# Two stored blocks to a product and a shorter ring of gathers in the second layer of a relational graph network

## The chip, the cores and the metric

The kernel runs on one core of one Trainium2 chip. The metric is the device time of one execution in microseconds (us). A profile is one execution taken by the hardware profiler. The core's engines work side by side and wait for each other through semaphores: TensorE (PE; PEld is its loading of weights), VectorE (DVE), ScalarE (ACT), GpSimd (POOL), and SyncE (SP), which only issues transfers here. POOL issues the indirect transfers, the gathers.

## The reference

12,500 nodes with 128 features, 200,000 edges sorted by their destination. An edge's relation, one of ten, is the argmax of ten of its attributes. Each of two layers takes, for each node and relation, the mean of the features of the edges' sources, projects it with the relation's matrix, adds the ten, and adds the projected node itself and a bias. The result is added to x and normalised.

```
def _rgcn_layer(x, src, dst, edge_type, w_rel, root, bias):
    seg = dst * NUM_REL + edge_type
    sums = segment_sum(x[src], seg, N * NUM_REL)
    cnt = segment_sum(ones, seg, N * NUM_REL)
    mean = (sums / maximum(cnt, 1.0)[:, None]).reshape(N, NUM_REL, -1)
    return einsum('nrd,rdo->no', mean, w_rel) + x @ root + bias
h = relu(_rgcn_layer(x, src, dst, edge_type, w_rel1, root1, b1))
out = layernorm(x + _rgcn_layer(h, src, dst, edge_type, w_rel2, root2, b2))
```

## The kernel before

Edges are taken in 1563 tiles of 128, in the order of their destinations. For a tile, POOL gathers the 128 source rows by an indirect transfer (`gathered`, L833), DVE builds a one-hot matrix with the edges' weights (`hots`, L840), PE multiplies the two into PSUM, and DVE adds the result to a running accumulator at a register's offset.

Layer 1 walks all tiles (products at L1077, additions at L866). As blocks of 256 nodes are finished, it writes their rows, projected with layer 2's ten matrices, to YD, and their features to hT. While it goes it also sums, for edges whose source's layer-1 row is ready, layer 2's sums by relation; they are stored for each block in SD. Its gathers of two rows at once use four buffers of four places each: the ring is 16 tiles long and is refilled in pieces of four.

Layer 2 (`layer_2`) handles the remaining edges from the projected rows in YD: 177 plain tiles, and 678 tiles of edges brought together from all over by a sort on the chip (`brought_together`, `listed`), whose steps are interleaved with the 177 plain tiles as jobs due at a tile's number. The tiles are walked in bunches of up to four. For bunch p the program emits, in this order: one-hots for bunch p + 3 (AH), blocks to be begun (`begun`, the product with root, L1499), gathers of the bunch (L833), its products (L1607), with a call of `between.run` after each tile's product, jobs, the additions of bunch p - 2 (L1637), and finished blocks (`finish`: transposes L1540, norm L773 to L783, rows out). Each engine executes its part in that order.

Two things inside this walk matter here.

The ring of gathers: `gathers` has six buffers of GQ = 8 places, so 48 tiles. Each time eight tiles have been gathered, the next buffer is taken. The order of places within a buffer is turned round at every second use, so that the first gather of a buffer waits for the last product that read it; that one wait covers the eight.

The stored sums: a block of 256 nodes whose sums are in SD is called heavy; there are 46. For each, `seen_in` loads SD's ten slices into one of two `held` tiles (L1513, issued by SP), and `seen` spreads ten products, one a relation, over the walk (L1521, up to 256 columns, into the one PSUM bank `alone`), then adds the bank to the layer's accumulator (L1528). A heavy block takes 12 tiles of the walk: products at 0 to 6, the addition at 9. The load for the block after the next is issued when the tenth product is done. A block is finished only when its tiles are done and its stored sums are added.

Of the kernel before, what the change touches and what calls it, by code (L numbers as in the profile page):

```python
# [21 lines left out]
NREL = 10  # L22
# [7 lines left out]
QB = 4  # L30
GB = 6
OB = 7
GQ = 8
# [13 lines left out]
BN = 2 * P  # L47
# [5 lines left out]
LAST = 40  # L53
READY = 5
NEAR = 4
GAPW = 112
LOW = 1 << 13
TOPN = (1 << 14) - 1
# [10 lines left out]
def rgcn_resnorm_kernel(ctx: ExitStack, tc: tile.TileContext, x, src, dst, attr, w_rel1, root1, b1,  # L69
# [7 lines left out]
    nc = tc.nc  # L77
# [130 lines left out]
    groups2, u = [], 0  # L208
    while u < NT2:
        n, w = group_at(u, UX if u < UX else NT2)  # L210
# [15 lines left out]
    SD = dram.tile([C, NREL, N], F32, name="SD")  # L226
# [8 lines left out]
    gathers = [lasting.tile([P, GQ * C], F32, name=f"g{i}") for i in range(GB)]  # L235
# [4 lines left out]
    def next_of(kind, of):  # L240

        turn_of_[kind] += 1
        return of[(turn_of_[kind] - 1) % len(of)]
# [98 lines left out]
    at = [0]  # L342
# [15 lines left out]
    first = float(chunk_rows(NCH - 1) * P) - 0.5  # L358
# [13 lines left out]
    n = chunk_rows(NCH - 1)  # L372
# [124 lines left out]
    wsb, rsb, bsb = [], [], []  # L497
# [635 lines left out]
    for a in range(0, NREL * RW, YB):  # L1133
        m = min(NREL * RW - a, YB)
# [33 lines left out]
    every = cc.rearrange("p l r n -> p (l r n)")  # L1168
# [250 lines left out]
    def layer_2():  # L1419
# [53 lines left out]
        heavy = [k for k in finals if block(k)[0] + block(k)[1] > first_sum]  # L1473
        opening = issued[plain - AH]
        due_at = [issued[max(0, first_at[k] - AH - 2)] for k in range(NB2)]
        for j, k in enumerate(heavy):
            due_at[k] = min(due_at[k], opening + 12 * j - 12)
        begin = sorted(range(NB2), key=lambda k: (due_at[k], k))
        xs = [comp.tile([P, 2, C], F32, name=f"x{i}") for i in range(3)]
        vs = [every[:, FIRST - 4 * BN:FIRST - 3 * BN].rearrange("p (t c) -> p t c", c=C)]  # L1480
        os_ = [comp.tile([P, 2, C], F32, name=f"o{i}") for i in range(2)]
        hs = [every[:, FIRST - (i + 1) * BN:FIRST - i * BN] for i in range(3)]
        held = [every[:, i * NREL * BN:(i + 1) * NREL * BN].rearrange("p (r n) -> p r n", r=NREL) for i in range(2)]
        turn_of_.update(x=0, v=0, o=0, h=0, sd=0)
        xbs, fTs, sds = {}, {}, {}
        whole, alone = set(), []
# [16 lines left out]
        def rows_in_turn(j):  # L1503
            if j < NB2:
                xbs[finals[j]] = next_of("x", xs)
                rows_dma(xbs[finals[j]], x, finals[j], False)

        def seen_in(j):
            if j < len(heavy):
                k = heavy[j]  # L1510
                n0, n, _ = block(k)
                sds[k] = next_of("sd", held)
                nc.sync.dma_start(sds[k][:, :, :n], SD[:, :, n0:n0 + n])  # L1513

        def seen(j, i):
            k = heavy[j]
            n0, n, _ = block(k)
            po = alone[0]

            def one(r):  # L1520
                nc.tensor.matmul(po[:, :n], wsb[1][:, r, :], sds[k][:, r, :n], start=(r == 0), stop=(r == NREL - 1))  # L1521
                if r == NREL - 1:
                    sds.pop(k)
                    seen_in(j + 2)

            def added(_):
                assert k in begin[:begins]
                nc.vector.tensor_tensor(acc2[:, n0:n0 + n], acc2[:, n0:n0 + n], po[:, :n], op=ALU.add)  # L1528
                whole.add(k)
            for r in range(NREL):  # L1530
                between.at(i + 2 * r // 3, lambda _, r=r: one(r))
            between.at(i + 9, added)

        def finish(j):
            k = finals[j]
# [24 lines left out]
        used_ = {}  # L1560
# [5 lines left out]
        for p in range(-AH, NB + BE):  # L1566
            if p == plain - AH:
                assert wanted[0] in ready
                masking.close()
                ps_n = fast.enter_context(tc.tile_pool(name="ps_n", bufs=1, space=PSUM))  # L1570
                banks[:] = [next_of("zp", banks) for _ in banks] + [ps_n.tile([P, YB], F32, name=f"zq{j}") for j in range(2)]
                turn_of_["zp"] = 0
                alone.append(ps_n.tile([P, YB], F32, name="alone"))
                for j in range(len(heavy)):
                    seen(j, i + 6 + 12 * j)
            if p + AH < NB:
                second, t0, n, w = bunches[p + AH]
                keys, weights = (keyB, wB) if second else (keyE, wE)
# [9 lines left out]
            if p < NB:  # L1588
                second, t0, n, w = bunches[p]
                oh = ohs.pop(p)  # L1590
                zps[p] = zp = next_of("zp", banks)
                for j in range(n):
                    if made % GQ == 0:
                        g = next_of("g", gathers)
                        turn = used_[id(g)] = 1 - used_.get(id(g), 1)
                    at = GQ - 1 - made % GQ if turn else made % GQ
                    made += 1
                    t = t0 + j
                    if second:
                        gathered(g, at, YD[:, :], idxB[:, t:t + 1], 1)  # L1600
                    else:
                        gathered(g, at, YD[:NREL * (limit_of(t) + 1), :] if t >= T0 else YD[:, :], idxE[:, t:t + 1], 1)
                    gs[j] = g, at
                for j in range(n):
                    g, at = gs.pop(j)
                    o = 0 if second else j * w
                    nc.tensor.matmul(zp[:, o:o + w], g[:, at * C:(at + 1) * C], oh[:, j * w:(j + 1) * w],  # L1607
                                     start=not second or j == 0, stop=not second or j == n - 1)
                    between.run(issued[p] + j + 1)
                i = issued[p + 1]  # L1610
# [204 lines left out]
```

## Time and profile before

| | us |
|---|---|
| runs (median of 3) | 3691.79 (3684.78 to 3692.25) |
| profiled execution | 3655.59 |
| its span | 3653.8 |
| POOL busy in the span | 2294.6 (63%) |
| PE busy in the span | 2254.1 (62%) |
| DVE busy in the span | 1994.0 (55%) |
| mean granted TensorE clock | 0.753 |

A row of the profile names the line, the engine, the operation, the tile written and those read, and the shape; behind it, the count and the times. In a timeline the first two numbers are the start and the length in us; a bracket gives how long the engine stood idle before, and what ended that ("issue": nothing that the profile shows; "remote": something that it could not tell). A product of float32 leaves two records. A gather is POOL's record DMA_INDIRECT; its length is that of the issue, not of the transfer.

### The profile page before, as it was taken

The page shows a single profiled execution, that of the slowest core. Times are in us where ns is not written, and L with a number is a line of the kernel's source. Part 1 is how long each engine was busy: PE and PEld are TensorE (multiplying, and loading weights), DVE is VectorE, ACT ScalarE, POOL GpSimd, SP SyncE. Part 2 cuts the span into 40 slices and gives each one's busy share as a digit, 9 for nine tenths or more (in the row PEclk, how much of TensorE's full clock was granted, in tenths as well). Part 3 has the DMA queues.
Part 4 walks back from the last instruction along what each step waited for, and adds up shares of the span by engine and source line. Part 5 has one row for each costly group of instructions (what it writes and reads, how often), then busy time and mean ns, then how long its engine had stood idle before and what let it go on. Part 6 is the DMA issues. An engine that isn't in the chain of part 4 may idle for free. (4 is left out here: it accounts for less than half of the span.)

```text
span 3653.8 us, 38569 instructions
## 1 busy us (share of the span) xinstructions
PE 2254.1 (62%) x11125; PEld 1859.4 (51%) x11125; DVE 1994.0 (55%) x6434; ACT 514.6 (14%) x799; POOL 2294.6 (63%) x2430
## 2 busy tenths in 40 slices
PE   1556677677676767676667667733556566566534
PEld 0445565565555555555555555623445555555433
DVE  4646576867565757565656565428654333233333
ACT  1111121212121212122212121100000000000000
POOL 5663666666666666666666666566566666666664
PEclk7677877878888888887888877855667777677655
DMA  4553656555555555555656555531144444444322
GB/s 122 154 170 96 189 155 192 153 186 165 172 172 169 172 177 176 171 182 158 191 159 194 158 161 157 146 98 51 46 117 135 143 137 140 136 151 135 97 61 51
DMA packets 376423, 529.31 MB, mean 145 GB/s; under 512 B 55904, under 2 KB 283707, under 8 KB 376204
## 3 DMA queue, kind: packets, MB, share of 16 engines
q0 software_dynamic: 99552, 249.45, 23.9%
q1 hardware_dynamic: 249209, 264.48, 22.4%
q10 hardware_dynamic: 27443, 12.82, 1.2%
q8 instruction: 93, 1.52, 0.2%
q14 instruction: 126, 1.03, 0.1%
HBM read 372.75 MB, written 160.19 MB: 146 GB/s over the span
## 5 line engine op out<-in xcount | busy, mean ns | idle before, releaser
L833 POOL DMA_INDIRECT g<-XH,idxE x1386 | 1314.1, 948 | 737.7 <-issue 364.8
L1077 PEld LDWEIGHTS zp<-oh,g 128*128 128x128 f32 x5898 | 901.7, 229 | 407.3 <-DVE cc L866 201.5
L1077 PE MATMUL zp<-oh,g 128*128 128x120 f32 x5898 | 943.1, 317 | 247.3 <-DVE cc L866 159.0
L866 DVE TENSOR_TENSOR cc<-cc,zp 128x240 f32 (+1 forms) x1563 | 607.1, 388 | 787.1 <-remote 353.0
L833 POOL DMA_INDIRECT g<-YD,idxB x678 | 642.6, 948 | 339.8 <-issue 185.9
L934 PE MATMUL yb<-w,a 128*128 128x512 f32 (+1 forms) x576 | 345.2, 689 | 346.0 <-ACT ys L940 183.1
L840 DVE TENSOR_SCALAR oh<-bank,keyE,wE 128x120 f32<-128x120 f32 x1563 | 517.7, 394 | 0.0
L1521 PE MATMUL alone<-cc,w 128*128 128x256 f32 (+2 forms) x920 | 339.4, 485 | 136.4 <-DVE cc L1528 72.8
L1607 PEld LDWEIGHTS zy<-oh,g 128*128 128x128 f32 x1168 | 245.9, 273 | 222.5 <-DVE cc L1637 155.1
L1607 PE MATMUL zy<-oh,g 128*128 128x12 f32 (+30 forms) x1168 | 237.2, 330 | 197.3 <-DVE cc L1637 148.2
L940 ACT ACTIVATE ys<-yb 128x512 f32<-128x512 f32 (+2 forms) x291 | 153.0, 526 | 1334.4 <-remote 553.7
L934 PEld LDWEIGHTS yb<-w,a 128*128 128x128 f32 x576 | 110.8, 240 | 379.1 <-ACT ys L940 203.6
L1521 PEld LDWEIGHTS alone<-cc,w 128*128 128x128 f32 x920 | 195.3, 247 | 158.3 <-DVE cc L1528 76.5
L826 PE MATMUL pf<-cc,w 128*128 128x256 f32 (+2 forms) x1040 | 248.4, 396 | 15.1 <-issue 9.2
L833 POOL DMA_INDIRECT g<-in_x_dram,idxE x177 | 167.8, 948 | 135.7 <-PE zp L1077 59.3
L833 POOL DMA_INDIRECT g<-YD,idxE x177 | 168.6, 953 | 111.1 <-issue 60.6
L826 PEld LDWEIGHTS pf<-cc,w 128*128 128x128 f32 x1040 | 205.7, 212 | 49.3 <-issue 19.8
L795 ACT ACTIVATE cc<-zero 128x1280 f32<-128x1280 f32 x170 | 214.6, 1262 | 0.0
L840 DVE TENSOR_SCALAR oh<-columns,keyB,wB 128x45 f32<-128x45 f32 (+35 forms) x678 | 177.0, 336 | 0.2 <-issue 0.2
L1637 DVE TENSOR_TENSOR cc<-cc,zy 128x12 f32 (+24 forms) x306 | 58.9, 192 | 177.8 <-remote 145.5
L1607 PEld LDWEIGHTS zq<-oh,g 128*128 128x128 f32 x542 | 113.2, 258 | 30.8 <-issue 18.4
L1528 DVE TENSOR_TENSOR cc<-cc,alone 128x256 f32<-128x256 f32 (+2 forms) x46 | 18.6, 405 | 199.3 <-remote 159.0
(265 smaller groups left out, 1563.5 us busy)
## 6 DMA issues: line engine op xcount, KB each, us to landing
SD<-cc SPq DMA_DIRECT2D x41, 1280.0 KB
cc<-SD SPq DMA_DIRECT2D x41, 1280.0 KB
YD<-ys SPq DMA_DIRECT2D x194, 256.0 KB
m<-in_edge_attr_dram SPq DMA_DIRECT2D x48, 672.0 KB
g<-XH,idxE POOLq DMA_INDIRECT x1386
YD<-ys SPq DMA_DIRECT2D x97, 128.0 KB
XH<-hb SPq DMA_DIRECT2D x44, 256.0 KB
g<-YD,idxB POOLq DMA_INDIRECT x678
```

The costliest lines, as they stand in the source:

```text
L795: nc.scalar.activation(cc[:, l, h * H:(h + 1) * H, o:o + n], zero[:, None, :n].to_broadcast([P, H, n]), AF.Copy)
L826: nc.tensor.matmul(po[:, :n], wsb[l][:, r, :], sums[:, r], start=(r == 0), stop=(w is None and r == NREL - 1))
L833: nc.gpsimd.indirect_dma_start(out=g[:, j * C:(j + n) * C], out_offset=None, in_=table, in_offset=bass.IndirectOffsetOnAxis(ap=idx, axis=0))
L840: nc.vector.tensor_scalar(oh[:, j * m:(j + 1) * m], cols[:, :m], keys[:, j:j + 1], weights[:, j:j + 1], op0=ALU.is_equal, op1=ALU.mult)
L866: nc.vector.tensor_tensor(s, s, z, op=ALU.add)
L934: nc.tensor.matmul(yb[:h, :m], fin_a[k][:, b * P:b * P + h], wsb[1][:, r:r + m // C, :], start=True, stop=True)
L940: nc.scalar.activation(ys[:h, :m], yb[:h, :m], AF.Copy)
L1077: nc.tensor.matmul(zp[:, o + l * KW:o + (l + 1) * KW], g[:, (slot[j] + l) * C:(slot[j] + l + 1) * C], oh[:, j * KW:(j + 1) * KW], start=Tr ...
L1521: nc.tensor.matmul(po[:, :n], wsb[1][:, r, :], sds[k][:, r, :n], start=(r == 0), stop=(r == NREL - 1))
L1528: nc.vector.tensor_tensor(acc2[:, n0:n0 + n], acc2[:, n0:n0 + n], po[:, :n], op=ALU.add)
L1607: nc.tensor.matmul(zp[:, o:o + w], g[:, at * C:(at + 1) * C], oh[:, j * w:(j + 1) * w], start=not second or j == 0, stop=not second or j = ...
L1637: nc.vector.tensor_tensor(s, s, zps[q][:, j * w:(j + 1) * w], op=ALU.add)
```

## The change

In layer 2, adjacent heavy blocks are put into groups of up to 512 columns whose first tiles lie less than 60 apart. One load of SD, ten products and one addition now serve a group; `held` tiles are twice as wide. A group takes 24 tiles of the walk: products at 0 to 13, the addition at 19. And the gathers use only the first two buffers, each as two pieces of four places: the ring is 16 tiles long and is refilled in pieces of four, with the same turning of the order.

```
+PACE = 24
+APART = 60
...
-        for j, k in enumerate(heavy):
-            due_at[k] = min(due_at[k], opening + 12 * j - 12)
+        pairs = []
+        for k in sorted(heavy, key=lambda k: block(k)[0]):
+            if pairs and block(pairs[-1][0])[0] + 2 * BN >= sum(block(k)[:2]) and first_at[k] - first_at[pairs[-1][0]] < APART:
+                pairs[-1].append(k)
+            else:
+                pairs.append([k])
+        pairs.sort(key=lambda u: min(finals.index(k) for k in u))
+        for j, u in enumerate(pairs):
+            for k in u:
+                due_at[k] = min(due_at[k], opening + PACE * j - 12)
...
-        held = [every[:, i * NREL * BN:(i + 1) * NREL * BN].rearrange("p (r n) -> p r n", r=NREL) for i in range(2)]
+        held = [every[:, 2 * i * NREL * BN:2 * (i + 1) * NREL * BN].rearrange("p (r n) -> p r n", r=NREL) for i in range(2)]
...
+        def span_of(j):
+            return block(pairs[j][0])[0], sum(block(k)[1] for k in pairs[j])
...
             def one(r):
-                nc.tensor.matmul(po[:, :n], wsb[1][:, r, :], sds[k][:, r, :n], start=(r == 0), stop=(r == NREL - 1))
+                nc.tensor.matmul(po[:, :n], wsb[1][:, r, :], sds[j][:, r, :n], start=(r == 0), stop=(r == NREL - 1))
...
             for r in range(NREL):
-                between.at(i + 2 * r // 3, lambda _, r=r: one(r))
-            between.at(i + 9, added)
+                between.at(i + 3 * r // 2, lambda _, r=r: one(r))
+            between.at(i + PACE - 5, added)
...
-                for j in range(len(heavy)):
-                    seen(j, i + 6 + 12 * j)
+                for j in range(len(pairs)):
+                    seen(j, i + 6 + PACE * j)
...
-                    if made % GQ == 0:
-                        g = next_of("g", gathers)
-                        turn = used_[id(g)] = 1 - used_.get(id(g), 1)
-                    at = GQ - 1 - made % GQ if turn else made % GQ
+                    if made % QB == 0:
+                        m = made // QB % NEAR
+                        g, first = gathers[m // 2], m % 2 * QB
+                        turn = used_[m] = 1 - used_.get(m, 1)
+                    at = first + (QB - 1 - made % QB if turn else made % QB)
```

More of the change, by code (lines that the diff above doesn't have):

```diff
@@ L1482, in layer_2 @@
         hs = [every[:, FIRST - (i + 1) * BN:FIRST - i * BN] for i in range(3)]
-        held = [every[:, i * NREL * BN:(i + 1) * NREL * BN].rearrange("p (r n) -> p r n", r=NREL) for i in range(2)]
+        held = [every[:, 2 * i * NREL * BN:2 * (i + 1) * NREL * BN].rearrange("p (r n) -> p r n", r=NREL) for i in range(2)]
+        assert 4 * NREL * BN <= FIRST - 4 * BN
         turn_of_.update(x=0, v=0, o=0, h=0, sd=0)
@@ L1506, in rows_in_turn @@
                 rows_dma(xbs[finals[j]], x, finals[j], False)
+        def span_of(j):
+            return block(pairs[j][0])[0], sum(block(k)[1] for k in pairs[j])
         def seen_in(j):
[L1509 to L1513, printed above, removed]
+            if j < len(pairs):
+                n0, n = span_of(j)
+                sds[j] = next_of("sd", held)
+                nc.sync.dma_start(sds[j][:, :, :n], SD[:, :, n0:n0 + n])
         def seen(j, i):
-            k = heavy[j]
-            n0, n, _ = block(k)
+            n0, n = span_of(j)
             po = alone[0]
             def one(r):
-                nc.tensor.matmul(po[:, :n], wsb[1][:, r, :], sds[k][:, r, :n], start=(r == 0), stop=(r == NREL - 1))
+                nc.tensor.matmul(po[:, :n], wsb[1][:, r, :], sds[j][:, r, :n], start=(r == 0), stop=(r == NREL - 1))
                 if r == NREL - 1:
-                    sds.pop(k)
+                    sds.pop(j)
                     seen_in(j + 2)
             def added(_):
-                assert k in begin[:begins]
+                assert all(k in begin[:begins] for k in pairs[j])
                 nc.vector.tensor_tensor(acc2[:, n0:n0 + n], acc2[:, n0:n0 + n], po[:, :n], op=ALU.add)
-                whole.add(k)
+                whole.update(pairs[j])
             for r in range(NREL):
-                between.at(i + 2 * r // 3, lambda _, r=r: one(r))
-            between.at(i + 9, added)
+                between.at(i + 3 * r // 2, lambda _, r=r: one(r))
+            between.at(i + PACE - 5, added)
         def finish(j):
```

## The prediction

> **What bounds the kernel now.** I read the table by stage first (columns after the two times: length, then busy us and instruction count of PE, PEld, DVE, ACT and POOL, granted clock, DMA share, GB/s). Layer 2 begins at about 2361 us, after a stage of layer 1 that is quoted last, of the gathers alone.
>
> ```profile
> 2387.00:2450.00 63.00, 19.01 (x71) 14.52 (x71) 10.48 (x40) 4.23 (x18) 42.46 (x45) 0.50 0.42 104
> 2450.00:2613.00 163.00, 63.25 (x262) 56.75 (x262) 127.64 (x318) 5.01 (x8) 107.03 (x112) 0.51 0.19 51
> 2613.00:2690.00 77.00, 49.17 (x210) 40.72 (x210) 52.92 (x247) 3.46 (x9) 42.95 (x46) 0.69 0.29 83
> 2690.00:2890.00 200.00, 123.05 (x573) 104.45 (x571) 87.02 (x392) 7.87 (x20) 127.56 (x135) 0.76 0.45 133
> 2890.00:3490.00 600.00, 354.01 (x1620) 308.71 (x1620) 186.57 (x812) 20.93 (x56) 391.45 (x414) 0.71 0.44 130
> 3490.00:3591.00 101.00, 37.65 (x163) 34.31 (x162) 32.67 (x147) 2.07 (x7) 67.36 (x71) 0.50 0.24 62
> ...
> 400.00:1500.00 1100.00, 708.91 (x749) 0.82 0.55 173
> ```
>
> No engine is full, but POOL's count hardly moves: 600/414 = 1.449 us per gather in the long stage with stored products, 101/71 = 1.42 behind it, where PE has half the work. So products do not set the pace; gathers do. Next, POOL's own timeline: the first gather after each pause (layer 2, then the tail, then layer 1, where gathers already go 16 ahead in pieces of four).
>
> ```profile
> 2945.91 0.94 POOL L833 DMA_INDIRECT g<-YD,idxB  x1 [3.30 <-remote]
> 2968.93 0.95 POOL L833 DMA_INDIRECT g<-YD,idxB  x1 [3.24 <-remote]
> ...
> 3522.89 0.95 POOL L833 DMA_INDIRECT g<-YD,idxB  x1 [4.27 <-remote]
> 3556.92 0.95 POOL L833 DMA_INDIRECT g<-YD,idxB  x1 [4.30 <-remote]
> ...
> 488.74 0.94 POOL L833 DMA_INDIRECT g<-XH,idxE  x1 [1.92 <-PE zp L1077]
> 500.45 0.95 POOL L833 DMA_INDIRECT g<-XH,idxE  x1 [1.99 <-PE pf L996]
> ...
> 1527.70 0.94 POOL L833 DMA_INDIRECT g<-XH,idxE  x1 [2.86 <-PE zp L1077]
> 1545.11 0.94 POOL L833 DMA_INDIRECT g<-XH,idxE  x1 [2.69 <-PE zp L1077]
> ```
>
> Between pauses a gather starts every 1.25 us. The runs are 16 gathers in 2968.93 - 2945.91 = 23.02 us (1.439 each), 24 in 34.03 (1.418), 8 in 11.71 (1.464), 12 in 17.41 (1.451). The pause grows with the run: 2.0, 2.7, 3.3, 4.3 us for 8, 12, 16, 24. So a longer run buys almost nothing, and a shorter one costs almost nothing: the whole scale from 8 to 24 is 3%.
>
> What is the pause? Beside it, other engines stand still and start together:
>
> ```profile
> 2957.50 0.64 PE L1521 MATMUL alone<-cc,w 128*128 128x256 f32 x2
> ...
> 2968.64 0.52 SPq L1513 DMA_DIRECT2D cc<-SD  x1
> 2968.65 0.42 DVE L1528 TENSOR_TENSOR cc<-cc,alone 128x256 f32<-128x256 f32 x1 [12.15 <-remote]
> ```
>
> The last stored product of that block has its record at 2957.50 to 2958.14, yet the DVE addition and the SP load that wait for it start at 2968.6, 0.3 us before POOL resumes. I read it so: while POOL issues without a pause, PE's completions reach the others late, and the pause lets them through. The Trainium skill ("Perfetto Trace Analysis", section "Per-instruction lifecycle: what the profiler-reported window actually captures") says that a TensorE end in a trace is an estimate and that the semaphore comes later; that fits the direction, but it names no delay of 10.5 us, so I take the size from these rows.
>
> Gathers are not late:
>
> ```profile
>   DMA g<-YD,idxB: 7.8, 6
> ```
>
> That row of L1607's waits says that PE's gather matmuls waited 7.8 us in all for data. At 1.25 us each, even 12 gathers of lead are 15 us.
>
> **The change part by part.** (1) The stored sums. From the kernel's constants and the diff's rule the 46 stored blocks make 22 groups of 512 columns (one of 468), at 24 tiles each instead of 12. So 460 products become 220, 46 additions 22, 46 SP loads 22 of twice the size; the last group is added near tile 696 instead of 722 of 855, and no group is later than the tiles its blocks wait for anyway. Prices, per record, two records to a product:
>
> ```profile
> L1521 PE MATMUL alone<-cc,w 128*128 128x256 f32 x820 | 309.6, 492 | 128.7 <-DVE cc L1528 72.8 <-issue 52.9 <-DVE oh L840 3.0
> L934 PE MATMUL yb<-w,a 128*128 128x512 f32 x384 | 258.9, 763 | 192.2 <-issue 101.8 <-ACT ys L940 87.8 <-ACT a L745 1.6
> L1528 DVE TENSOR_TENSOR cc<-cc,alone 128x256 f32<-128x256 f32 x41 | 17.1, 418 | 174.3 <-remote 143.0 <-PE alone L1521 14.1 <-PE pf L1540 10.0
> ```
>
> PE: 2 x 492 against 763 ns saves 0.22 us per record, times 440 records is 97 us of PE time at most (records overlap; clocks differ), and nothing at least. DVE: an addition of 512 columns lies between 0.42 and 0.84 us, 22 of them between 9 and 18 us against 17.1. Both lie beside POOL, which has 1.45 us per gather to itself; if that cover were gone, PE's share would be the gain. The wait of the next group's first product for the one bank is no worse: addition and next product are five tiles apart, before three. I take 2 us gained, in 2690 to 2890, where POOL falls to 200/135 = 1.48; bounds 0 and 7 (135 x 0.05). The doubled loads take about twice the time, beside gathers that have 15 us to spare, and the first two have 36 us until the first product:
>
> ```profile
> 2648.42 1.50 SPq L1513 DMA_DIRECT2D cc<-SD  x2
> ...
> 2684.35 2.05 PE L1521 MATMUL alone<-cc,w 128*128 128x256 f32 x4
> ```
>
> A rule of the Trainium skill ("TensorE: Matmul & The Clock Gate", "Why this matters for your kernels") asks for no idle gaps over about 3 us between matmul bursts, lest the clock fall to half; longer products would serve it. The granted clock was 0.71 in the long stage and 0.50 in the tail, where POOL was faster, so by the trace the clock buys nothing here.
>
> (2) Steady pace. With a ring of 16 in pieces of four a run can have 4 to 16 gathers. Layer 1 has that ring and shows mostly 8 and 12; here PE's load per gather is less, so I take 12: 1.451. After 2690 there are 135 + 414 = 549 gathers at 1.439 and 94 (71 in the row above and the last 23) at 1.418: 549 x 0.012 + 94 x 0.033 = +10 us. Bounds: runs stay 16 (+2); layer 1's mean, 1100/749 = 1.469 against 1.449 and 1.418 (+16).
>
> (3) The opening. Here the long lead acts.
>
> ```profile
> 2386.81 0.95 POOL L833 DMA_INDIRECT g<-YD,idxE  x1 [11.16 <-issue]
> ...
> 2441.99 0.95 POOL L833 DMA_INDIRECT g<-YD,idxE  x1 [0.30 <-issue]
> 2450.39 0.94 POOL L833 DMA_INDIRECT g<-YD,idxE  x1 [7.46 <-remote]
> ...
> 2624.41 0.95 POOL L833 DMA_INDIRECT g<-YD,idxE  x1 [11.59 <-PE zy L1607]
> ...
> 2403.19 0.76 DVE L1637 TENSOR_TENSOR cc<-cc,zy 128x12 f32 x4
> 2410.74 0.77 DVE L1637 TENSOR_TENSOR cc<-cc,zy 128x12 f32 x4 [6.00 <-remote]
> 2449.93 0.57 DVE L1637 TENSOR_TENSOR cc<-cc,zy 128x12 f32 x3 [37.58 <-remote]
> ...
> 2387.00:2450.00 63.00, 8.27 (x38) 8.95 (x38) 0.50 0.42 104
> 2450.00:2613.00 163.00, 49.46 (x216) 47.47 (x216) 0.51 0.19 51
> 2613.00:2690.00 77.00, 16.99 (x98) 17.47 (x98) 0.69 0.29 83
> ```
>
> (The last three are the stage table of L1607 alone, PE and PEld.) POOL, 11 tiles ahead already, runs 45 gathers without a pause, and DVE stands 37.58 us at the third addition: the longest such stand of the trace. PE has done 19 tiles by 2450, 127 by 2613, 176 by 2690; POOL has issued 56, 168 and 214. A ring of 16 stops POOL after five more gathers. What is lost: it can be at most 16 beyond PE and DVE. What is gained: pauses come every 4 to 12 gathers, so the chain DVE, PE, ACT, PE, DVE of the sorting is held about 6 us at a hop instead of 10 to 20; I let DVE pass its third addition at 2430, 20 us sooner, with tile 14 done. From there the pace is POOL's, 1.446: tile 127 at 2430 + 113 x 1.446 = 2593. The stretch behind it took 77 us for 49 tiles, more than POOL's pace, and I leave it so: tile 176 at 2670, POOL at about 190; at 2690 it has 204, against 214. Ten gathers at 1.46 are **+15 us**. Bounds: the stand goes entirely (DVE on at 2412: 216 gathers, -3 us); nothing is gained (2690 with 190 gathers: +35).
>
> (4) The end.
>
> ```profile
> 3618.57 0.94 POOL L833 DMA_INDIRECT g<-YD,idxB  x1 [0.30 <-issue]
> ...
> 3622.04 0.42 DVE L773 TENSOR_TENSOR cc<-pf,x 128x256 f32<-128x256 f32 x1 [22.52 <-remote]
> ...
> 3639.42 0.47 PE L1607 MATMUL zq<-oh,g 128*128 128x26 f32 x2
> ...
> 3620.00:3654.00 34.00, 11.27 (x50) 11.25 (x50) 0.50 0.14 32
> ```
>
> POOL ends at 3619.5, the span at 3653.8: 34.3 us. After the pause (about 3 us) PE and DVE had 25 tiles left (the last row: L1607's 50 records behind 3620), to 3639.9, and then 14 us of last blocks. With at most 16 behind, most of them done in the last run, I take 3 + 5 + 14 = 22: **-12 us** (bounds -6, if eight more tiles are left, and -16, if none).
>
> The waits at the head of each piece are now twice as many, on POOL; behind them stand only later gathers, which the rows above price as the pauses.
>
> Sum: 15 + 10 - 12 - 2 = +11 us on the profiled execution's 3655.6 (its span is 3653.8), 3667 us. The runs have a median of 3691.8, 1% above the profiled one; I add the 11 us to the median: **3703 us**.
>
> **The rivals.** (a) The opening is freed: the third addition comes by 2412 and the 49 tiles take under 75 us, because each hop waits less. Then (3) gives -3 to -14 (tile 176 at 2640 at the earliest, the pace of POOL alone), the rest -4 to -10: 3668 to 3685, say 3676, faster. For it: 37.58 us is one stand, and a pause of 11.59 us, POOL waiting for PE, lies in the last stretch. Against: DVE is busy 127.64 of 163 us behind it, which no shorter run takes away. It decides when POOL at 2690 has issued over 210 gathers. (b) Start and end cancel: (3) at +8, (2) at +4, (4) at -12: 3692. (c) Short runs: if products of 512 columns hold PE so that a run has only four gathers, each costs about 1.25 + 1/4 = 1.50, and 643 x 0.06 = +39 with the opening +15 and the end -12: 3734. Against: layer 1, with more work per gather, shows 8 and 12. (d) PE does set the pace where POOL has 1.48 and 1.57 to 1.67 (77/46), so that cheaper products gain there: 7 + 10 us, and with (3) at 0: 3680. By the clock page above this would be larger still; the tail speaks against it. (e) The lead does not do what it says, because the wait at a piece's head never was what stopped POOL: no change, 3692. The pauses after exact multiples of eight speak against it.
>
> **How the numbers follow.** Forecast 0.38; (c) 0.06; (b) 0.22; (e) 0.04; (a) 0.25; (d) 0.05. About 0.2% (7 us) is what a measurement of this kernel can tell from no change. Slower 0.44, same 0.26, faster 0.30. The forecast's own range, by its bounds, is 3680 to 3725; for 8 in 10 I need (a) and (b) and a part of (c): 3668 to 3735.
>
> **What would show it.** POOL's runs: 8 or 12 gathers between pauses of 2 to 2.7 us in the long stage, 1.45 to 1.465 per gather; at 1.44 or less step (2) is wrong. DVE's longest stand in the opening under 20 us; at 30 or more the tie between POOL's runs and PE's completions is wrong. POOL's gathers issued by 2690: 204 forecast. From POOL's last gather to the end 22 us. About 440 records of 512 columns at L1521's place, and a PE share that falls without the pace changing; a pace that changes with it would mean (d).

## The result, and the profile after

The changed kernel takes 3675.28 us (median of 4 runs, 3671.15 to 3678.59); the kernel before, beside it, takes 3690.79 (4 runs, 3684.78 to 3692.25). The ratio is 0.9952, 95% interval 0.9938 to 0.9965: 15.5 us less. The forecast was 3703, slower. One execution of the changed kernel in a later session (l2 below) took 4770.4 us at a granted clock of 1.00 where the others had 0.75; it is counted in no ratio.

One thing has to be known before the traces are read. The profiled execution of before (3655.6) came, as far as the traces tell, from another session than its three timed runs: layer 1 hands over to layer 2 at 2361 us there and at 2397 us in the profile of after, and of these 36 us only 5.9 are a longer wait of POOL just before the hand-over. So positions in layer 2 are counted here from its first gather, not from the span's start. This is POOL's timeline of before, first and last gather of layer 2 (the last one is quoted in the prediction, at 3618.57):

```profile
2361.36 0.95 POOL L833 DMA_INDIRECT g<-YD,idxE  x1 [3.94 <-PE zp L1077]
```

and of after, the same two:

```profile
2397.14 0.94 POOL L835 DMA_INDIRECT g<-YD,idxE  x1 [9.79 <-PE zp L1079]
...
3648.26 0.94 POOL L835 DMA_INDIRECT g<-YD,idxB  x1 [0.30 <-issue]
```

Before, layer 2 lasts 3653.8 - 2361.4 = 1292.4 us, of which 35.2 lie behind the start of the last gather. After, it lasts 3670.2 - 2397.1 = 1273.1, of which 22.0 lie there. So 13.2 of these 19.3 us are in the drain. The other 6.1 come before it, but POOL's wait ahead of the first gather is 5.9 us longer after (9.79 against 3.94). Where that boundary is put decides whether the walk itself gained anything, and the groups of POOL's gathers, which count that wait too, say that it did not. The columns are busy us, mean ns, idle us before them and what ended it. Before:

```profile
L833 POOL DMA_INDIRECT g<-YD,idxB x678 | 642.6, 948 | 339.8 <-issue 185.9 <-remote 97.8 <-PE zy L1607 33.7
L833 POOL DMA_INDIRECT g<-YD,idxE x177 | 168.6, 953 | 111.1 <-issue 60.6 <-PE zy L1607 31.9 <-remote 10.5
```

After:

```profile
L835 POOL DMA_INDIRECT g<-YD,idxB x678 | 640.3, 944 | 342.4 <-issue 190.7 <-remote 84.1 <-PE zy L1620 34.4
L835 POOL DMA_INDIRECT g<-YD,idxE x177 | 168.2, 951 | 110.8 <-issue 62.7 <-PE zy L1620 19.7 <-remote 18.6
```

Busy and idle together are 1262.1 us before and 1261.7 after. A ring of a third of the length costs POOL nothing in that pair of profiles, in the opening (idxE) as in the rest (idxB).

The table by stage of after answers to the first fence of the prediction, row by row, each 36 us later (columns as there: PE, PEld, DVE, ACT, POOL, granted clock, DMA share, GB/s; layer 1 first):

```profile
400.00:1500.00 1100.00, 765.51 (x3960) 621.25 (x3959) 722.42 (x2210) 221.50 (x302) 696.62 (x737) 0.82 0.55 171
2423.00:2486.00 63.00, 33.73 (x142) 29.53 (x141) 42.51 (x115) 5.40 (x19) 41.77 (x43) 0.50 0.35 89
2486.00:2649.00 163.00, 80.48 (x343) 69.52 (x344) 125.07 (x372) 5.00 (x11) 101.94 (x108) 0.59 0.25 74
2649.00:2726.00 77.00, 42.64 (x149) 28.49 (x149) 43.23 (x213) 3.25 (x9) 46.30 (x49) 0.63 0.35 108
2726.00:2926.00 200.00, 133.02 (x467) 83.58 (x467) 77.70 (x339) 6.80 (x18) 129.52 (x137) 0.75 0.44 140
2926.00:3526.00 600.00, 352.60 (x1231) 224.77 (x1230) 180.79 (x782) 19.42 (x55) 391.88 (x415) 0.70 0.39 120
3526.00:3627.00 101.00, 48.96 (x152) 36.03 (x152) 35.55 (x157) 2.06 (x7) 65.09 (x69) 0.50 0.23 59
```

POOL has 415 gathers in the long stage against 414, and 69 in the tail against 71: the pace has not moved. DVE works 42.51 us in the first stretch of the opening, where it worked 10.48, and PE 33.73 instead of 19.01. What has moved is where PE stands. Two windows of after, PE's gather products alone (L1620), from the first gather to the place where layer 2 was at 2690 before, and from the end of the last issue on:

```profile
2397.10:2725.70 328.60, 84.62 (x406) 85.75 (x406) 0.60 0.32 92
...
3649.20:3670.20 21.00, 1.91 (x6) 1.57 (x6) 0.50 0.20 35
```

and POOL's gathers in the first of them, after:

```profile
2397.10:2725.70 328.60, 205.10 (x216) 0.60 0.32 92
```

With two records to a tile, PE has done 203 of 216 issued tiles, where it had done 176 of 214 before; behind the last issue it has 3 tiles left instead of 25. One row of the waits of L1620 tells the same of the whole layer: PE now stands waiting for gathers, 283.1 us where it was 7.8 (products and weight loads added up, which wait side by side; the products alone 126.5).

```profile
  DMA g<-YD,idxB: 283.1, 323
```

### The profile page after: what moved, and what is told of

Same layout as the page of the kernel before. It is cut to its first block, busy times and chain, and to the rows that moved or that the text cites. A ratio compares the mean times of both kernels' runs of the same rounds, so it can differ in the third digit from the quotient of the medians.

```text
span 3670.2 us, 37654 instructions
## 1 busy us (share of the span) xinstructions
PE 2319.0 (63%) x10645; PEld 1779.5 (48%) x10645; DVE 1991.3 (54%) x6410; ACT 511.8 (14%) x799; POOL 2287.4 (62%) x2430
## 5 line engine op out<-in xcount | busy, mean ns | idle before, releaser
L1079 PEld LDWEIGHTS zp<-oh,g 128*128 128x128 f32 x5898 | 918.4, 234 | 396.5 <-DVE cc L868 180.1
L1079 PE MATMUL zp<-oh,g 128*128 128x120 f32 x5898 | 957.0, 320 | 228.6 <-DVE cc L868 132.3
L936 PE MATMUL yb<-w,a 128*128 128x512 f32 (+1 forms) x576 | 354.9, 706 | 383.3 <-ACT ys L942 229.0
L1620 PEld LDWEIGHTS zy<-oh,g 128*128 128x128 f32 x1168 | 244.8, 275 | 317.9 <-DVE cc L1650 119.1
L1620 PE MATMUL zy<-oh,g 128*128 128x12 f32 (+30 forms) x1168 | 258.4, 347 | 206.5 <-DVE cc L1650 114.6
L1533 PE MATMUL alone<-cc,w 128*128 128x512 f32 (+1 forms) x440 | 305.3, 782 | 31.6 <-issue 16.9
L775 DVE TENSOR_TENSOR cc<-pf,x 128x256 f32<-128x256 f32 (+2 forms) x52 | 21.2, 409 | 358.9 <-remote 219.9
L1620 PEld LDWEIGHTS zq<-oh,g 128*128 128x128 f32 x542 | 110.8, 253 | 151.2 <-DMA g<-YD,idxB 74.0
L1620 PE MATMUL zq<-oh,g 128*128 128x45 f32 (+33 forms) x542 | 122.9, 341 | 84.3 <-DMA g<-YD,idxB 59.5
```

Source lines behind the costliest of these rows:

```text
L775: nc.vector.tensor_tensor(v[:p, s], pr[:p, s], xb[:p, s], op=ALU.add)
L936: nc.tensor.matmul(yb[:h, :m], fin_a[k][:, b * P:b * P + h], wsb[1][:, r:r + m // C, :], start=True, stop=True)
L1079: nc.tensor.matmul(zp[:, o + l * KW:o + (l + 1) * KW], g[:, (slot[j] + l) * C:(slot[j] + l + 1) * C], oh[:, j * KW:(j + 1) * KW], start=Tr ...
L1533: nc.tensor.matmul(po[:, :n], wsb[1][:, r, :], sds[j][:, r, :n], start=(r == 0), stop=(r == NREL - 1))
```

## The experiments

Theory L, from which I set out: the short lead makes the gain, because less is left behind the last gather. Its rivals: P, the cheaper products make it; S, the smaller pieces make it. Each kernel was profiled, and timed in 5 rounds beside the kernel before; a session is the runs that were made together. "The drain" is the time from the start of POOL's last gather to the end.

**The first session: parts alone.** e1 has the pairs with the old ring; its edit to the changed kernel:

```
-                    if made % QB == 0:
-                        m = made // QB % NEAR
-                        g, first = gathers[m // 2], m % 2 * QB
-                        turn = used_[m] = 1 - used_.get(m, 1)
-                    at = first + (QB - 1 - made % QB if turn else made % QB)
+                    if made % GQ == 0:
+                        g = next_of("g", gathers)
+                        turn = used_[id(g)] = 1 - used_.get(id(g), 1)
+                    at = GQ - 1 - made % GQ if turn else made % GQ
```

> The pairs of stored blocks, with the ring of 48 gathers in pieces of eight as before. Theory L (the short lead makes the gain, because less is left to do behind the last gather): from POOL's last gather to the end stays 33 to 37 us, and the time is that of before less 0 to 4 us (ratio 0.999 to 1.000). Rival P (the cheaper products make it): 10 to 17 us less, ratio 0.995 to 0.997, with fewer microseconds per gather between gathers 214 and 854 of layer 2 (1.43 or less against 1.449).

e2 is before with the reverse of that edit.

> The ring of 16 gathers in pieces of four, with the 46 stored blocks one at a time as before. Theory L: from POOL's last gather to the end falls to 20 to 25 us, and the time is 11 to 17 us under before (ratio 0.9955 to 0.997). Rival P: 0 to 5 us under before. If the products of 256 columns hold PE so that POOL's runs shrink (my step 2), it is slower than the changed kernel by 5 us or more.

e3 is the changed kernel with

```
-                        m = made // QB % NEAR
+                        m = made // QB % (2 * GB)
```

> The changed kernel, but its ring is 12 pieces of four, 48 gathers. Theory L: the lead is long again, PE ends some 25 to 35 gathers behind, the drain is 30 to 37 us, and the time lies 0 to 5 us under before. Rival S (pieces of four that come free sooner make the gain, however long the ring): 11 to 17 us under before, as the changed kernel.

e4 is the changed kernel itself.

> The changed kernel again, beside the others on the same chip. Both theories: 12 to 19 us under before (ratio 0.995 to 0.997). The span of layer 2, from its first gather to the end, is 1270 to 1277 us, whatever layer 1 takes in that execution.

Measured: before 3072.5 us, 17% less than in the runs above, and the order turned round. Pairs alone 3071.7 (ratio 1.0001, 0.9992 to 1.0009); long ring in fours 3071.6 (0.9996, 0.9987 to 1.0004); ring alone 3097.5 (1.0084, 1.0071 to 1.0097); the changed kernel 3094.2, **slower** (1.0072, 1.0060 to 1.0084). The times of e1 and e3 are those of theory L, those of e2 and e4 are not, and the drain is 18 us in all four. Layer 1 is shorter too, so it is the session that differs. The reason stands in POOL's groups, here of e1:

```profile
L835 POOL DMA_INDIRECT g<-YD,idxB x678 | 640.9, 945 | 206.6 <-issue 199.3 <-DMA g<-YD,idxB 2.4 <-PE zq L1619 1.5
L835 POOL DMA_INDIRECT g<-YD,idxE x177 | 167.8, 948 | 57.3 <-issue 53.0 <-DMA g<-YD,idxE 2.1 <-PE zy L1619 1.2
```

and of e4:

```profile
L835 POOL DMA_INDIRECT g<-YD,idxB x678 | 641.1, 946 | 206.6 <-issue 189.9 <-DMA g<-YD,idxB 9.1 <-PE zy L1620 3.0
L835 POOL DMA_INDIRECT g<-YD,idxE x177 | 167.5, 946 | 82.3 <-issue 54.3 <-PE zy L1620 22.6 <-PE zp L1079 2.8
```

An issue takes the 0.945 us that it took before, but the pauses behind runs are gone: 206.6 us of idle time for 678 gathers is 0.305 each, the step between two issues. The time is then that of the gathers, 1.25 us apiece. I call such a session free, and one as in the first traces (1.45 apiece, idle time that "remote" ended) held. In a free session the whole loss of the short ring is in the opening, 82.3 - 57.3 = 25.0 us of idle time, and none later (2.5 of it is the wait ahead of the first gather). POOL's timeline of e4, the gathers behind a pause there:

```profile
2155.07 0.94 POOL L835 DMA_INDIRECT g<-YD,idxE  x1 [0.92 <-PE zy L1620]
2165.07 0.94 POOL L835 DMA_INDIRECT g<-YD,idxE  x1 [5.32 <-PE zy L1620]
2178.43 0.94 POOL L835 DMA_INDIRECT g<-YD,idxE  x1 [8.69 <-issue]
2201.33 0.94 POOL L835 DMA_INDIRECT g<-YD,idxE  x1 [3.20 <-PE zy L1620]
```

At that place PE waits for DVE's additions, which stand behind the sort's steps, and is then taken by the sort's products (L1317). PE's timeline of e1 there:

```profile
2152.20 1.88 PE L1619 MATMUL zy<-oh,g 128*128 128x12 f32 x8 [8.43 <-DVE cc L1649]
2154.97 8.16 PE L1317 MATMUL pf<-cc 127*128 127x256 f32 x24 [0.89 <-issue]
...
2168.38 6.99 PE L1317 MATMUL pf<-cc 127*128 127x256 f32 x18 [4.23 <-DVE li L1341]
```

e1's ring rides over this jam: by 2155.5 us POOL has issued 141 gathers and PE done 123 tiles, in the next 30 us 24 and 12, so the lead goes from 18 to 30; 150 us later it is 2, without POOL having stopped. These are the rows (PE's tiles from L1619's records, two each; then POOL's gathers):

```profile
1975.50:2155.50 180.00, 56.72 (x246) 0.54 0.34 90
2155.50:2185.50 30.00, 2.98 (x24) 0.80 0.24 62
2185.50:2335.50 150.00, 49.36 (x295) 0.83 0.54 176
```

```profile
1975.50:2155.50 180.00, 133.71 (x141) 0.54 0.34 90
2155.50:2185.50 30.00, 22.74 (x24) 0.80 0.24 62
2185.50:2335.50 150.00, 113.66 (x120) 0.83 0.54 176
```

That gave theory J: the long ring pays only over the jam, the short one only at the end of a held session.

**The second session (held, before 3688.0): the ring by parts of the layer.** f1 keeps 48 up to gather 216 and then 16, f2 the other way round:

```
-                        m = made // QB % NEAR
+                        q = made // QB
+                        m = q % (2 * GB) if q < 54 else (54 + (q - 54) % NEAR) % (2 * GB)
```

```
-                        m = made // QB % NEAR
+                        q = made // QB
+                        m = q % NEAR if q < 56 else (q - 52) % (2 * GB)
```

> The changed kernel with the ring of 48 for the first 216 gathers of layer 2 and the ring of 16 behind them. Theory J (the long ring pays only over the jam near tile 127, where sorting holds PE and VectorE for some 35 us; the short one pays only at the end, and only on a chip where POOL pauses behind each run of gathers): on a chip without the pauses the time of before (ratio 0.999 to 1.001, the 22 us of the changed kernel gone), on a chip with them 9 to 16 us under before, with 20 to 25 us from the last gather to the end. Rival A (the short ring costs or gains all along layer 2): on a chip without the pauses 10 us or more over before.

> The changed kernel with the ring of 16 for the first 224 gathers of layer 2 and the ring of 48 behind them. Theory J: on a chip without the pauses 20 to 25 us over before, as the changed kernel (ratio 1.0065 to 1.0085); on a chip with them 0 to 5 us under before, with 33 to 37 us from the last gather to the end. Rival A: on a chip without the pauses 5 to 12 us over before.

f1 takes 3691.7 us, 3.7 over before (ratio 1.0010, 0.9998 to 1.0022), though its drain is 18.3 us; f2 takes 3681.7, 6.3 under (0.9985, 0.9971 to 1.0000), drain 30.8. Theory J fell with f1. Its POOL timeline, where the ring shrinks, shows why:

```profile
2737.57 0.95 POOL L835 DMA_INDIRECT g<-YD,idxB  x1 [7.92 <-PE zy L1621]
2743.45 0.95 POOL L835 DMA_INDIRECT g<-YD,idxB  x1 [1.18 <-issue]
2773.55 0.95 POOL L835 DMA_INDIRECT g<-YD,idxB  x1 [25.41 <-PE zy L1621]
```

POOL stands 25.41 us until PE has worked off the lead. What is saved in the drain has been paid here. That is theory D: in a held session PE is some 38 tiles behind from the opening on (176 of 214 at 2690 in before), it never catches up while the ring is long, and these tiles are a debt that POOL or the end must wait for wherever the lead is given up.

f2 shows that the debt need not come from the opening. Its ring is 16 there, and at gather 216 PE has done 203 tiles. These are the rows of the 71.5 us behind that, in which the long ring opens, and of the 800 us that follow (PE's records of L1621, two to a tile; then POOL's gathers):

```profile
2725.50:2797.00 71.50, 8.10 (x48) 0.66 0.31 93
2797.00:3597.00 800.00, 202.19 (x1118) 0.69 0.39 121
```

```profile
2725.50:2797.00 71.50, 49.23 (x53) 0.66 0.31 93
2797.00:3597.00 800.00, 519.05 (x550) 0.69 0.39 121
```

POOL issues 53 gathers while PE does 24 tiles, so the lead goes from 13 to 42, and 800 us later it is still 33: the long ring filled, in a held session, within 72 us of being opened, and PE did not catch up.

**The third session (free, before 3070.6).** g1 is before with `next_of("g", gathers[:2])` for `next_of("g", gathers)`: 16 gathers in pieces of eight. g2 is e1 once more. g3 has `m = made // QB % 8`, a ring of 32. g4 has the long ring up to gather 780:

```
-                        m = made // QB % NEAR
+                        q = made // QB
+                        m = q % (2 * GB) if q < 195 else (195 + (q - 195) % NEAR) % (2 * GB)
```

> Before with one edit: its pieces of eight go round two buffers instead of six, so the ring is 16 gathers; the stored blocks stay single. Theory D (on a chip where POOL pauses behind each run of gathers, the lead is a debt: the 48 are spent in the opening, where VectorE stands, PE never comes closer than some 30 gathers, and these are paid back behind the last gather): on such a chip 10 to 18 us under before (ratio 0.995 to 0.997), with 18 to 24 us from the last gather to the end; on a chip without pauses 15 to 30 us over. Rival P (the pairs make the gain): 0 to 4 us under before on the first chip. Rival S (it takes pieces of four): the same, 0 to 4 us under, or slower.

> The pairs alone, the ring of 48 in pieces of eight as before (the kernel of e1, for a chip where POOL pauses). Theory D: 0 to 4 us under before, layer 2 1286 to 1294 us long, 31 to 36 us from the last gather to the end. Rival P: 10 to 17 us under before. On a chip without the pauses: the time of before, as in e1.

> The changed kernel with a ring of 8 pieces of four, 32 gathers. Theory D: on a chip with the pauses the debt is 16 smaller than with 48 and 16 larger than with 16, so the drain is 25 to 30 us and the time 5 to 11 us under before. On a chip without pauses the ring covers most of the jam near tile 127, where the long ring's lead rises to 30: 0 to 4 us over before. Rival A (any ring longer than 16 is as good as 48): on a chip with the pauses 0 to 3 us under before.

> The changed kernel with the ring of 48 up to gather 780 of layer 2 and the ring of 16 for the last 75. Theory D: the debt is paid where the ring shrinks instead of behind the last gather; POOL stands there for 8 to 20 us, the drain is 18 to 24 us, and on a chip with the pauses the time is 0 to 6 us under before. Rival E (only the drain matters, and shortening the lead at the last moment is enough): 10 to 15 us under before. On a chip without pauses: the time of before, within 3 us.

g1 takes 29.3 us more than before (ratio 1.0096, 1.0082 to 1.0109), some 4 more than e2 did with pieces of four; g2 is level (1.0008, 0.9999 to 1.0017), g4 too (1.0001, 0.9991 to 1.0010); g3 takes 7.3 more (1.0022, 1.0012 to 1.0031), against the 0 to 4 expected: 32 places don't quite cover the jam. In its profile POOL stands there once, 3.6 us for PE at its 173rd gather (as in k2 below), where no kernel with 48 places stands; the rest of the 7.3 us is not accounted for. For held sessions this one says nothing.

**The fourth session (held, before 3653.9).** h1 is e1, h2 is e2.

> The pairs alone, the ring of 48 in pieces of eight as before, wanted from a session where POOL pauses behind each run of gathers (before at 3685 to 3692). There theory D (the lead is a debt, the products lie beside POOL): 0 to 4 us under before, layer 2 1286 to 1294 us long, 31 to 36 us from the last gather to the end; rival P (the cheaper products make the gain): 10 to 17 us under. In a session without the pauses (before at 3070): the time of before within 3 us.

> The ring of 16 in pieces of four alone, the 46 stored blocks single as before, wanted from a session with the pauses. There theory D: 10 to 17 us under before (ratio 0.9955 to 0.9975), 18 to 24 us from the last gather to the end; rival P: 0 to 5 us under; if products of 256 columns shorten POOL's runs, 5 us or more behind the changed kernel. In a session without the pauses: 22 to 28 us over before.

The ring alone gains what theory D said: 3639.8 us, 14.2 under before (ratio 0.9960, 0.9942 to 0.9979), drain 18.2. So the gain does not need the pairs, and rival P falls. The pairs alone take 3669.0, 15.1 **over** before (1.0040, 1.0021 to 1.0059), which neither theory had. The profile can't tell where: that execution, at 3648.2, is the fastest of its twelve, and in it POOL's layer 2 is as long as that of before and the drain is 27.8.

**The fifth session (free, before 3072.0)**, meant for the two open questions, repeated the third: k1 is g4, k2 is g3, k3 the changed kernel, k4 is e1.

> The changed kernel with the ring of 48 up to gather 780 of layer 2 and of 16 for the last 75, in a session with the pauses. Theory D (the lead is a debt that is paid where it is given up): 0 to 6 us under pairs alone (k4), the drain 18 to 24 us, and POOL standing some 8 to 20 us where the ring shrinks. Rival E (only the drain matters): 10 to 15 us under k4. In a session without the pauses: the time of before within 3 us.

> The changed kernel with a ring of 32 gathers, in a session with the pauses. Theory D: half the debt, the drain 24 to 29 us, and a time half way between k4 and k3 (within 5 us). Rival A (any ring longer than 16 is as good as 48): within 3 us of k4. In a session without the pauses: 5 to 9 us over before, as in g3.

> The changed kernel again. In a session with the pauses, theory D: 11 to 18 us under before (ratio 0.995 to 0.997) and within 4 us of the gain of the ring alone (h2, 14 us). If the 15 us that the pairs cost alone are a cost of the pairs whatever the ring, it is no faster than before. In a session without the pauses: 20 to 24 us over before.

> The pairs alone again. Theory D: the time of before within 5 us in a session with the pauses; the 15 us over before of h1 would then be a spread of that session's runs. If it is 10 to 20 us over before once more, the pairs cost something beside the long ring, and the profile has to show in which part of layer 2.

Ratios: k1 0.9998 (0.9988 to 1.0007), k2 1.0020 (1.0011 to 1.0029), k3 1.0070 (1.0058 to 1.0083), k4 0.9992 (0.9984 to 1.0001).

**The sixth session (held, before 3690.7).** l1 is g4, l2 the changed kernel.

> The changed kernel with the ring of 48 up to gather 780 of layer 2 and of 16 for the last 75, in a session with the pauses. Theory D (the lead is a debt that is paid where it is given up): no better than 6 us under before, the drain 18 to 24 us, and POOL standing 8 to 20 us longer than usual where the ring shrinks. Rival E (only the drain matters): 10 to 15 us under before. In a session without the pauses: the time of before within 3 us.

> The changed kernel again, in a session with the pauses. Theory D: 11 to 18 us under before, layer 2 1265 to 1276 us long, and within 4 us of the gain of the ring alone (h2, 14 us). If the pairs cost 15 us whatever the ring (as h1 alone would have it), it is no faster than before. In a session without the pauses: 20 to 24 us over before.

l2 takes 3672.5, 18.2 under before (ratio 0.9954, 0.9939 to 0.9968): the result again. l1 takes 3684.9, 5.8 under (0.9985, 0.9976 to 0.9995), with a drain of 22.0. The rival that only the drain matters (E) wanted 10 to 15. Of the two, run beside each other, l1 is 12.3 us behind l2, from which it differs only in the ring's length up to gather 780: the pieces of four and the pairs are the same, and the drains are 22.0 and 21.5. So neither the drain alone nor the small pieces (rival S) make the gain. POOL's timeline of l1 has the payment, where the ring shrinks:

```profile
3534.79 0.94 POOL L835 DMA_INDIRECT g<-YD,idxB  x1 [5.99 <-PE zq L1621]
3572.99 0.94 POOL L835 DMA_INDIRECT g<-YD,idxB  x1 [13.43 <-PE zy L1621]
3595.95 0.94 POOL L835 DMA_INDIRECT g<-YD,idxB  x1 [3.21 <-PE zy L1621]
```

The held profiles side by side. The second column is the idle time of POOL before the 855 gathers, the sum of the two groups of each profile; medians are against before in their own session.

| kernel | idle, us | drain, us | sum against before | median against before |
|---|---|---|---|---|
| before | 450.9 | 35.2 | 0 | 0 |
| changed | 453.2 | 22.0 | -10.9 | -15.5 |
| changed (l2) | 459.0 | 21.5 | -5.6 | -18.2 |
| ring alone (h2) | 450.9 | 18.2 | -17.0 | -14.2 |
| 16 from gather 216 (f1) | 473.9 | 18.3 | +6.1 | +3.7 |
| 16 up to gather 224 (f2) | 454.1 | 30.8 | -1.2 | -6.3 |
| 16 for the last 75 (l1) | 460.2 | 22.0 | -3.9 | -5.8 |
| pairs alone (h1) | 454.4 | 27.8 | -3.9 | +15.1 |

One profile a row, of runs that spread by 7 to 36 us, so the sums follow the medians only roughly: l1's profile is that of its fastest execution, 8.2 us under its median, and h1's is 20.8 under. The medians are the evidence. The kernels whose ring is 16 throughout gain 14 to 18 us, and those that have it for a part gain 6 or lose 4. f1, f2 and l1 contain the pairs, so against before they carry whatever the pairs cost beside a long ring, which h1 leaves open; l1 against l2 does not. A ring of 16 in pieces of eight (g1) was not run in a held session.

The idle time also holds POOL's wait ahead of the first gather, and that is a cost of the change. These are the first gathers of h1 and of h2, one session, eights and fours:

```profile
2359.43 0.94 POOL L835 DMA_INDIRECT g<-YD,idxE  x1 [2.41 <-PE zp L1079]
2369.00 0.94 POOL L833 DMA_INDIRECT g<-YD,idxE  x1 [9.85 <-PE zp L1077]
```

All kernels in pieces of four wait 8.4 to 12.8 us here in held sessions and 2.6 to 6.5 in free ones, whether their ring has 16, 32 or 48 places; those in eights 2.4 to 3.9 and 0.3. Layer 1 gathers into the first four of the same buffers; the pieces of four always begin with the first of them, while the old ring went on in turn, so the wait for layer 1's products (zp) is probably this. No run began with another buffer.

## Why the prediction was wrong

**What bounds the kernel.** Right for the session it was read in: POOL's gathers and the pauses behind their runs set the pace, and neither products nor data do. That the pauses belong to the chip's session and not to the kernel I could not see in one trace.

**Step (3), the opening, +15: this step failed.** It gave POOL 204 gathers by 2690; it had 216 at the same distance from the first gather, against 214. What was mis-sized is how much of VectorE's stand the shorter runs take away. DVE's timeline of after, the third addition and the longest stand behind it in the opening:

```profile
2436.80 0.57 DVE L1650 TENSOR_TENSOR cc<-cc,zy 128x12 f32 x3 [1.22 <-PE zy L1620]
...
2448.32 1.68 DVE L1239 SCALAR_TENSOR_TENSOR cc<-cc,low,go 127x1408 f32<-127x1408 f32 x1 [8.63 <-issue]
```

The third addition comes 39.7 us behind the first gather; before it was 88.6, and I had let it be 68.6. PE's gather products of after (L1620), to tile 14, from there to tile 127, and to tile 176:

```profile
2397.10:2437.20 40.10, 5.80 (x28) 0.66 0.69 183
2437.60:2598.80 161.20, 51.50 (x226) 0.51 0.19 51
2598.80:2673.50 74.70, 17.68 (x98) 0.68 0.36 119
```

Tile 14 is done some 28 us sooner than forecast (40 us behind the first gather, not 68.6). The next 113 tiles take 161 us, where I had 163, and the 49 behind them 75, where I had 77. So the pace and the stretch behind it were right, and nearly the whole error sits in the one stand: I took 20 us off it, and 48.9 went. With PE so much sooner, a POOL that may be only 16 ahead of it loses nothing. And the old ring's 38 tiles of lead were not output. PE and DVE came sooner (203 tiles done instead of 176) while POOL, with the same pauses, issued as many, and the old ring was full when the jam came, so POOL stood there in both kernels: 11.59 us until 2624.41 before, and in after, where the profile names no releaser,

```profile
2611.75 0.94 POOL L835 DMA_INDIRECT g<-YD,idxE  x1 [8.34 <-issue]
```

In a free session the long ring still has room when the jam comes, and then the loss is real: 25.0 us of idle time, 22 to 25 us in the time of the kernels with the ring of 16 in fours. That is not what the +15 was derived from.

**Step (2), the pace, +10: wrong.** I took runs of 12, at 1.451. From gather 216 to the last, 639 gathers take 3648.26 - 2725.7 = 922.6 us, 1.444 each, against (3618.57 - 2690.0) / 641 = 1.449 before. The mis-sized part is the old price: I took it from one run of 16 (1.439), though the table by stage has 1.449 and 1.48 for the same 549 gathers. Against these, runs of 12 at 1.451 would have cost some 0 to 4 us, not 10. Counting as a pause all idle time over 1 us, before has 39 pauses in this part and after 45; the mean run fell from 16.4 to 14.2 gathers, and the pauses together are 137.6 and 138.8 us. Nor do runs end at 16 or stay at 12: PE now keeps within a few tiles, and, as I read it, a piece is often free when POOL comes to it. This is POOL's timeline of after, the heads of two runs:

```profile
2909.96 0.94 POOL L835 DMA_INDIRECT g<-YD,idxB  x1 [3.44 <-remote]
...
2938.76 0.94 POOL L835 DMA_INDIRECT g<-YD,idxB  x1 [4.14 <-remote]
```

That run has (2938.76 - 4.14 - 2909.96 + 0.30) / 1.25 = 20 gathers, at 1.44. The long stage as a whole has 600/415 = 1.446, under the 1.45 to 1.465 that I had named.

**Step (4), the end, -12: right.** The drain is 22.0 us, as forecast, against 35.2: -13.2. That f1 has the drain and not the gain, and l1 a third of it, shows what the step left out: it is a gain only because nothing was paid for it earlier.

**Step (1), the pairs, -2: neither shown nor refuted beside the short ring.** The changed kernel gains 15.5 and 18.2 us, the ring alone 14.2, with intervals of some 6 us either way; in three free sessions the pairs alone are at 1.0001, 1.0008 and 0.9992. The 15.1 us over before of h1 contradict it beside the long ring, and stay unexplained. Of the 97 us of PE time that I set as a bound, 34.1 came. The products' group on the page of after:

```profile
L1533 PE MATMUL alone<-cc,w 128*128 128x512 f32 (+1 forms) x440 | 305.3, 782 | 31.6 <-issue 16.9
```

and on the page of before, all shapes together:

```profile
L1521 PE MATMUL alone<-cc,w 128*128 128x256 f32 (+2 forms) x920 | 339.4, 485 | 136.4 <-DVE cc L1528 72.8
```

The saving lies beside POOL, and the pace did not follow it, as the step said. The sign that I named for it, a PE share that falls, did not come: over the whole of layer 2 PE is busy 719.1 us after and 689.8 before. The gather products, 1710 records in both, account for more than the difference (343.1 us before, 381.3 after); why stays open. The clock did not rise with the longer products: 0.70 in the long stage against 0.71, 0.50 in the tail in both. So the rule of the Trainium skill ("TensorE: Matmul & The Clock Gate", "Why this matters for your kernels"), by which fewer idle gaps would help, moved nothing here; no run here shows gaps shut altogether.

**The sum and the rivals.** The forecast terms were +15, +10, -2 and -12. In the two profiles the opening is 2 gathers ahead (-2.9), the 639 behind it 3.1 less for pace and pairs together, the end -13.2: -19.2, and -13.6 if POOL's longer wait ahead of the first gather is counted in. Rival (a) is the opening as it came: it asked for the third addition by 2412 (39.7 us behind the first gather is 2401 on before's scale), the 49 tiles in under 75 us (74.7) and over 210 gathers (216). That its 3676 is the median within 1 us is in part luck: it gave the opening 3 to 14 us and the rest 4 to 10, and the two profiles have 2.9 and 16.3. The sum of rival (d) does not come out: 7 + 10 us gained, (3) at 0, and (2) and (4) as forecast give 3673 and not 3680. And the range of 3680 to 3725 is narrower than the bounds of the four terms, which add up to 3668 to 3737. Adding the difference to the median of the runs, not to the profiled time, was right: in the profile of after, which is of the session that was timed, layer 1 takes some 30 us more.

## What to carry to other kernels

A lead of transfers is worth its depth only where it is still unspent when a jam comes; count, at the start and the end of each stage, how many are issued and how many are used up, and if the difference stays at the ring's length, the ring is a debt that the end pays. A shorter ring must be short from the first use to the last: shortening it later moves most of the payment (f1, l1), and lengthening it later builds the debt up again (f2). And before a change of less than one per cent is believed, it has to be run in more than one session: this one gains 0.5% in one kind and loses 0.7% in the other, and no version tried here is clearly the better in both. The one with 48 places up to gather 780 and 16 behind it comes nearest: it gains 0.15% in the held session (l1) and is level in two free ones (g4, k1). 32 places lose 0.2% in free sessions and were never run in a held one.

## What the runs showed of the hardware

Two kinds of sessions. In one (before at 3654 to 3691) a run of n back-to-back gathers ends in a pause of 2 to 4 us that grows with n, and engines that wait for PE start together with it. In the other (before at 3071 to 3073) POOL issues the 855 gathers of layer 2 at 1.25 us, if the ring has 48 places (e1). The length of an issue is the same, 0.945 us, in both; layer 1 has 878 gathers from 400 to 1500 us in e4, and 737 in the same kernel in a held session (above):

```profile
400.00:1500.00 1100.00, 857.80 (x4743) 687.57 (x4743) 844.59 (x2560) 265.02 (x364) 829.75 (x878) 0.89 0.65 203
```

The kernel does not decide which: the changed kernel and before were run in both. Nor does the chip's number: the chips listed as 4 and 11 each showed both. One difference stands on record: in the three free sessions four kernels were run beside before, in the three held ones two, and in that of the result one. Whether that is the cause or chance was not tried, and what makes a session held stays open.
